# Three one-element instructions behind the last output of a two-layer feed-forward kernel

## Chip, cores and metric

The kernel runs on one core of a Trainium2 chip. The metric is the device time of one execution in microseconds (us), the median over several runs.

## The reference

`x` has 8 sequences of 128 tokens with 512 features in float32. Two layers are applied, each a conditioning projection followed by a gated feed-forward network, with the result added to `x`:

```python
x = x + _L0_ffn_ref(_L0_cond_ref(x, itok_B_0_7, W, Wr, A, B), qweight_gu, ...)
x = x + _L1_ffn_ref(_L1_cond_ref(x, weight, itok_B_3_7), ln_w, gate_w, up_w, down_w)
```

In layer 0 the conditioning is `x @ W.T` plus a low-rank term whose 8 experts are weighted by a top-2 gate; its feed-forward network has weights of 4 bits with a scale per group, width 1376. In layer 1 each sequence picks one of 8 weight matrices, the result is normalized by its root mean square, and the feed-forward network has width 1792: `(silu(g) * u) @ down_w.T`. The output has the shape of `x`.

## The kernel before

Features lie on the 128 partitions and the 1024 tokens along the free axis, in two halves of 512 (`NTB = 2`, `TB = 512`); the 512 features make four chunks (`KC = 4`). The running `x` and the final result share one tile, `xT`. Float32 products are made of several products in a faster format: each operand is split into a high part, a low part and a difference, and the sums for the high and low parts and for the differences go to one PSUM bank, which is rescaled in between.

The whole network is written by `network_in`, which the program contains twice. `adaln_ffn_kernel` first calls it in the form that the inputs normally allow (`by_groups` true). During that, a one-element count decides whether the inputs were outside what this form can take; the answer is stored in `flag`, one column of a small tile (`told`, line 974, from the 1x1 product of `met`, line 971). Behind the first network stands a conditional block, `tc.If(again[0] > 0, ...)` on line 1719, that holds the second network, a general fallback. In the runs here the block is jumped over. Every engine loads the flag (line 1641) and has its own compare-and-branch instruction on line 1719. TensorE, VectorE and ScalarE (`FETCHED`) also get a hint of the coming jump when the last down projection begins (line 1642, shown in the profile under line 1876).

The order of layer 1's work is made ahead of time by a planner (`Plan`): tasks with keys, costs and engines are sorted into one order, and each task's function writes its instructions. The last tasks are those of `down`, called for the last block of the inner dimension (`last`). There `parts` lists the eight pieces of the output, (half, feature chunk), and the last one is cut into two of 256 columns, so that `i` runs from 0 to 8 and `i == NTB * KC` is the final piece. For each piece TensorE sums products into a bank (line 1628), ScalarE or VectorE rescales it (lines 1227 and 1229), TensorE adds more, and `done` lets VectorE add the bank to `x` (line 1685) and starts the output's DMA (lines 1690 and 1692). The DMA of the last piece but one is issued from ScalarE's queue, all others from SyncE's. Behind the last piece each engine has its jump, then one instruction that waits for its own semaphore's last value and adds to it what the skipped block would have counted (line 1719), and then the closing barrier (line 1876): SyncE waits for all semaphores, every engine reports to GpSimd, and GpSimd clears the semaphores and lets all go.

Of the kernel before, what the change touches and what calls it, by code (L numbers as in the profile page):

```python
# [14 lines left out]
F32 = mybir.dt.float32  # L15
F32R = mybir.dt.float32r
I32 = mybir.dt.int32
# [4 lines left out]
ALU = mybir.AluOpType  # L22

P = 128
# [3 lines left out]
NTB = NT // TB  # L28
NWARM = 36
KC = D // P  # L30
# [70 lines left out]
GU_PLACE, FLAG_PLACE, COND_PLACE = 64, 24, 48  # L101
# [31 lines left out]
class Plan:  # L133
# [5 lines left out]
    def add(self, name, engines, fn, deps=(), key=0.0, takes=(), gives=()):  # L139
        t = Task(name, engines, fn, deps, key, takes, gives)  # L140
        for d in t.deps:
            d.then.append(t)
        self.tasks.append(t)
        return t
# [67 lines left out]
        self.us = now  # L212


def network(tc: tile.TileContext, a, out, by_groups, flag=None, again=None):


    with ExitStack() as ctx:
        network_in(ctx, tc, a, out, by_groups, flag, again)


def network_in(ctx, tc, a, out, by_groups, flag, again):
    nc = tc.nc

    const = ctx.enter_context(tc.tile_pool(name="const", bufs=1, side="left"))
# [983 lines left out]
    def of(k, *who):  # L1209
        x = plan.place[k, who]  # L1210
        return late_tiles[x] if isinstance(x, tuple) else x

    def pe(us):
        return {"pe": us}
# [7 lines left out]
    def either(n):  # L1222
        return act(n) | dve(n)

    def scaled(engine, out_, in_, by):
        if engine == "act":
            nc.scalar.activation(out_, in_, AF.Copy, scale=by)  # L1227
        else:
            nc.vector.tensor_scalar(out_, in_, by, None, ALU.mult)
# [346 lines left out]
    def h_tile(j, tb):  # L1576
        x = of("h3", j, tb)
        return x if len(x.shape) == 3 else x.rearrange("p i n k -> p i (n k)")

    def down_weights(j, k):  # L1580
        raw = add(
            "wd", {"sp": 0.4}, lambda _: nc.sync.dma_start(out=of("wd", j), in_=a["wd1"][:, j, :]), [fd_open], k - 10.0,
            [("wd", (j,))],
        )

        def high(_):
            nc.scalar.activation(of("d", j)[:, 0], of("wd", j), AF.Copy, scale=HSCALE)

        def large(_):
            nc.scalar.activation(of("wd", j), of("wd", j), AF.Copy, scale=1.0 / EPS)  # L1590

        def low(_):
            d = of("d", j)
            nc.vector.scalar_tensor_tensor(d[:, 1], d[:, 0].bitcast(F32), -1.0 / EPS, of("wd", j), ALU.mult, ALU.add)

        def diff(_):
            d = of("d", j)
            nc.vector.tensor_tensor(d[:, 2], d[:, 0].bitcast(F32), d[:, 1].bitcast(F32), ALU.subtract)

        t0 = add("d hi", act(D), high, [raw], k, [("d", (j,))])  # L1600
        t1 = add("d large", act(D), large, [t0], k)
        t2 = add("d lo", dve(D), low, [t1], k, (), [("wd", (j,))])
        t3 = add("d di", dve(D), diff, [t2], k)
        d_ready[j] = (t0, t2, t3)

    def down(j0, j1):
        k, n = begin["down", j0], j1 - j0
        last = j1 == NJ1
        for j in range(j0, j1):
            down_weights(j, k - DOWN_LEAD + D_STEP * (j - j0))  # L1610
        users = []
        parts = [(tb, m, 0, TB) for tb in range(NTB) for m in range(KC)]
        if last:
            tb, m = parts.pop()[:2]
            parts += [(tb, m, c0, c0 + TB // 2) for c0 in (0, TB // 2)]
        for i, (tb, m, c0, c1) in enumerate(parts):
            kk = k + 3 * n * PASS * i
            who = ("down", j0, m, tb, c0)
            mine, t, w = [], None, c1 - c0
            one = PASS * w / TB + (0.007 if w < TB else 0.0)  # L1620

            d_first = last and i >= NTB * KC - 1
            first_key = k + 3 * n * PASS * (NTB * KC - 1) - D_FIRST
            firsts = (2, j0) if d_first else (0, j0)

            def products(j, which, m=m, tb=tb, who=who, c0=c0, c1=c1, firsts=firsts):
                for i in which:
                    nc.tensor.matmul(  # L1628
                        of("bank", *who)[:, : c1 - c0],
                        lhsT=of("d", j)[:, i, m * P : (m + 1) * P],  # L1630
                        rhs=h_tile(j, tb)[:, i, c0:c1],
                        start=((i, j) == firsts),
                        stop=True,
                        skip_group_check=(i, j) != firsts,
                    )

            def sums(t, key, takes=()):
                for j in range(j0, j1):
                    def high_low(_, j=j, products=products, tell=(last and i == 0 and j == j0)):
                        if tell and by_groups:  # L1640
                            again.append(nc.values_load(flag[:1, :], min_val=0, max_val=1))
                            tc.mark_branch_hint_location("again", hint=again[0], engines=FETCHED)
                        products(j, (0, 1))

                    t = add(
                        "down H", pe(2 * one), high_low, [*h_ready[j, tb][:2], *d_ready[j][:2], t], key,
                        takes if j == j0 else (),
                    )
                    mine.append((j, t))
                return t  # L1650

            def differences(t, key, some, takes=()):
                def fn(_, products=products):
                    for j in some:
                        products(j, (2,))

                needs = [x[2] for j in some for x in (h_ready[j, tb], d_ready[j])]
                t = add("down D", pe(len(some) * one), fn, [t, *needs], key, takes)
                mine.extend((j, t) for j in some)
                return t  # L1660

            def rescaled(t, by, key):
                def fn(e, who=who, w=w):
                    ps = of("bank", *who)[:, :w]
                    scaled(e, ps, ps, by)

                return add("rescale", either(w), fn, [t], key)

            takes = [("bank", who)]
            if d_first:  # L1670
                t = None
                for j in range(j0, j1):
                    t = differences(t, first_key, [j], takes if j == j0 else ())
                t = rescaled(t, DSCALE, first_key)
                t = sums(t, kk)
            else:
                t = sums(None, kk, takes)
                t = rescaled(t, HLSCALE, kk + R_AT)
                t = differences(t, kk + (DD_LAST if last and i == NTB * KC - 2 else DD_AT), range(j0, j1))
            by_end = 1.0 + EPS if d_first else -EPS  # L1680

            def done(_, i=i, m=m, who=who, by_end=by_end, cols=slice(tb * TB + c0, tb * TB + c1)):
                x = xT[:, m, cols]
                ps = of("bank", *who)[:, : cols.stop - cols.start]
                nc.vector.scalar_tensor_tensor(x, ps, by_end, x, ALU.mult, ALU.add)  # L1685
                if last:
                    by = nc.scalar if i == NTB * KC - 1 else nc.sync
                    if i == 1:
                        some = out[: 2 * P, cols].rearrange("(m p) t -> p m t", p=P)
                        by.dma_start(out=some, in_=xT[:, :2, cols])  # L1690
                    elif i > 1:
                        by.dma_start(out=out[m * P : (m + 1) * P, cols], in_=x)

            add("done", dve(w), done, [t], kk + DONE_AT, (), [("bank", who)])
            users += [(j, tb, t) for j, t in mine]
        for j in range(j0, j1):
            for tb in range(NTB):
                add("h3", {None: 0.0}, None, [t for jj, tt, t in users if (jj, tt) == (j, tb)], k, (), [("h3", (j, tb))])
            add("d", {None: 0.0}, None, [t for jj, _, t in users if jj == j], k, (), [("d", (j,))])
# [11 lines left out]
@with_exitstack  # L1711
def adaln_ffn_kernel(ctx: ExitStack, tc: tile.TileContext, a, out):
    nc = tc.nc

    outer = ctx.enter_context(tc.tile_pool(name="outer", bufs=1, side="right"))
    flag = outer.tile([P, FLAG_PLACE], I32, name="flag")[:, :1]
    again = []
    network(tc, a, out, True, flag, again)
    with tc.If(again[0] > 0, preferred_fallthrough_block=True, label="again", name="again"):
        network(tc, a, out, False)  # L1720


def hidden_order(w, axis):
# [157 lines left out]
```

## Time and profile before

| | before |
|---|---|
| median of 9 runs | 414.28 us (413.5 to 414.49) |
| profiled execution, its own time | 414.49 us |
| its span, first to last instruction | 412.6 us |
| TensorE busy | 405.9 us (98%) |
| VectorE busy | 368.2 us (89%) |
| ScalarE busy | 304.4 us (74%) |
| GpSimd busy | 29.0 us (7%) |
| granted TensorE clock, mean | 0.996 |
| last VectorE instruction (line 1685) | starts at 407.51 us, takes 0.42 us |

PE is TensorE (PEld its weight loads), DVE is VectorE, ACT is ScalarE, POOL is GpSimd, SP is SyncE. A "q" behind an engine's name marks its sequencer: waits, jumps and DMA issues, in which the engine itself does nothing. Times within an execution are in us from the first instruction. Times given to a hundredth are those of the trace's own records, where a view rounds to a tenth. The profile is of one execution; the time of that execution is its span and what lies around it, here 1.9 us.

### The profile page before, as it was taken

To read this page: it belongs to the slowest core of one execution; us is meant where nothing else is said; L and a number is where in the kernel's file an instruction comes from. 1 tells how busy PE (TensorE), PEld (TensorE's weight loads), DVE (VectorE), ACT (ScalarE), POOL (GpSimd) and SP (SyncE) were. 2 spreads that over 40 slices of the span, in tenths; PEclk is the share of its full clock that TensorE was granted. 3 is DMA by queue.
4 is the path that set the end of the run, shared out by engine and by line. 5 is a ranking of instruction groups with operands and counts; after the bars stand their busy time and mean duration, and the time that the engine had idled before them with its cause. 6 is when DMAs were issued, how large, how long until landed. Compare 5 with 4: busy or idle time off the path is not lost.

```text
span 412.6 us, 5202 instructions
## 1 busy us (share of the span) xinstructions
PE 405.9 (98%) x1779; PEld 320.2 (78%) x1779; DVE 368.2 (89%) x677; ACT 304.4 (74%) x502; POOL 29.0 (7%) x35
## 2 busy tenths in 40 slices
PE   9999999999999999999999999999999999999995
PEld 9886788888888867445778888888888888888884
DVE  3998989997999788988999999989999899988973
ACT  5843688958896786487999887867976688767751
POOL 1000200000000400421011011011011101000000
PEclk9999999999999999999999999999999999999998
DMA  8930830110010540682144114323323225000005
GB/s 286 396 145 2 246 85 3 49 45 14 0 64 2 184 147 2 244 305 50 51 154 78 64 25 128 92 36 91 113 54 91 73 46 138 0 2 1 25 2 209
DMA packets 17041, 38.59 MB, mean 94 GB/s; under 512 B 1904, under 2 KB 8944, under 8 KB 15984
## 3 DMA queue, kind: packets, MB, share of 16 engines
q1 hardware_dynamic: 11472, 25.09, 18.1%
q0 software_dynamic: 5104, 12.72, 12.2%
q10 hardware_dynamic: 432, 0.39, 0.3%
q8 instruction: 15, 0.25, 0.2%
q14 instruction: 18, 0.15, 0.1%
HBM read 36.10 MB, written 2.10 MB: 93 GB/s over the span
## 4 chain that ended last, share of the span: by engine, by line
PE 91%; DVE 5%; ACT 2%; issue 0%; DVEq 0%
PE bank L1480 30%; PE bank L1628 19%; PE down L731 9%; PE gate L681 9%; PE up L681 9%; PE bank L1292 6%; PE base L532 5%; PE experts L435 2%; PE base L558 2%; PE idle L388 1%; DVE xt L1260 1%; DVE a L1257 1%; PE bank L1333 1%; DVE down L315 1%; ACT h L337 0%
## 5 line engine op out<-in xcount | busy, mean ns | idle before, releaser
L1227 ACT ACTIVATE bank<-bank 128x512 f32<-128x512 f32 (+1 forms) x126 | 71.2, 582 | 23.6 <-PE bank L1480 14.0
L1628 PE MATMUL bank<-h,d 128*128 128x512 f32 (+1 forms) x249 | 67.3, 382 | 0.0
L1628 PEld LDWEIGHTS bank<-h,d 128*128 128x128 f32 x249 | 45.6, 188 | 9.2 <-DVE h L1105 0.2
L681 PE MATMUL gate<-a,dq 128*128 128x512 f32 (+1 forms) x176 | 47.7, 393 | 0.0
L681 PE MATMUL up<-a,dq 128*128 128x512 f32 (+1 forms) x176 | 47.4, 391 | 0.0
L1480 PE MATMUL bank<-a,w 128*128 128x512 f32 x168 | 45.2, 391 | 0.4 <-ACT snap L1227 0.4
L1480 PE MATMUL bank<-xs,w 128*128 128x512 f32 x168 | 44.3, 390 | 0.0
L731 PE MATMUL down<-h,wd 128*128 128x512 f32 (+1 forms) x176 | 41.6, 391 | 0.1
L731 PEld LDWEIGHTS down<-h,wd 128*128 128x128 f32 (+1 forms) x176 | 32.9, 188 | 7.9 <-DVE h L700 0.5
L681 PEld LDWEIGHTS gate<-a,dq 128*128 128x128 f32 (+1 forms) x176 | 32.5, 185 | 8.2 <-ACT gate L313 0.6
L681 PEld LDWEIGHTS up<-a,dq 128*128 128x128 f32 (+1 forms) x176 | 32.4, 185 | 7.9 <-DVE a L824 0.3
L1480 PEld LDWEIGHTS bank<-a,w 128*128 128x128 f32 x168 | 31.2, 188 | 7.8 <-ACT snap L1227 0.8
L313 ACT ACTIVATE gate<-gate,ratio 128x1024 f32<-128x1024 f32 (+1 forms) x26 | 28.2, 1085 | 11.4 <-PE gate L681 11.4
L1480 PEld LDWEIGHTS bank<-xs,w 128*128 128x128 f32 x168 | 31.4, 188 | 6.4
L1227 ACT ACTIVATE snap<-bank 128x512 f32<-128x512 f32 x42 | 25.1, 597 | 13.6 <-PE bank L1480 13.4
L1108 DVE SCALAR_TENSOR_TENSOR w<-w 128x512 fp32r<-128x512 f32 x50 | 34.3, 687 | 0.1
L1685 DVE SCALAR_TENSOR_TENSOR xT<-bank,xT 128x512 f32<-128x512 f32 (+1 forms) x41 | 27.5, 676 | 4.2 <-PE bank L1628 3.8
L1095 POOL DMA_DIRECT2D raw<-in_wgu x14 | 17.2, 1228 | 197.6 <-PE up L681 45.9
L1514 DVE SCALAR_TENSOR_TENSOR snap<-bank,snap 128x512 f32<-128x512 f32 x42 | 28.4, 688 | 2.1 <-PE bank L1480 2.0
L1628 PE MATMUL bank<-w,d 128*128 128x512 f32 x96 | 30.1, 389 | 0.0
L1105 DVE TENSOR_TENSOR w<-raw,w 128x512 fp32r<-128x512 f32 x42 | 28.7, 686 | 0.2 <-ACT w L1102 0.2
L1292 PE MATMUL bank<-w,xT 128*128 128x512 f32 x64 | 28.9, 594 | 0.0
(169 smaller groups left out, 743.0 us busy)
## 6 DMA issues: line engine op xcount, KB each, us to landing
raw<-in_wgu SPq DMA_DIRECT2D x13, 640.0 KB, 3.9
raw<-in_wgu POOLq DMA_DIRECT2D x14, 256.0 KB, 4.5
wd<-in_wd SPq DMA_DIRECT2D x14, 256.0 KB, 2.6
qw<-in_qw_gu SPq DMA_DIRECT2D x5, 512.0 KB, 4.0
xT<-in_xT SPq DMA_DIRECT2D x2, 1024.0 KB, 12.2
xb<-in_first SPq DMA_DIRECT2D x7, 256.0 KB, 4.8
out<-xT SPq DMA_DIRECT2D x5, 256.0 KB, 2.1
qwd<-in_qw_d SPq DMA_DIRECT2D x2, 512.0 KB, 9.4
```

The lines of the kernel that those rows point to most:

```text
L313: nc.scalar.activation(ps, ps, AF.Copy, scale=by)
L532: nc.tensor.matmul(base[m], lhsT=wT3[i][:, m, c * P : (c + 1) * P], rhs=x_parts(tb)[i][:, c, :], start=(i == 0 and c == 0), stop=(i == 1 a ...
L681: nc.tensor.matmul(ps, lhsT=dqs[j][:, c, half, :], rhs=a3[i][:, c, tb * TB : (tb + 1) * TB], start=(c == 0 and i == 0), stop=(i == 1), ski ...
L731: nc.tensor.matmul(ps[:, tb], lhsT=wds[k][:n, m * P : (m + 1) * P], rhs=h2[k][i][:, tb], start=(first and i == 0), stop=(i == 1), skip_gro ...
L1105: nc.vector.tensor_tensor(lo, raw, hi.bitcast(F32), ALU.subtract)
L1108: nc.vector.scalar_tensor_tensor(di, lo.bitcast(F32), -1.0 / EPS, hi.bitcast(F32), ALU.mult, ALU.add)
L1227: nc.scalar.activation(out_, in_, AF.Copy, scale=by)
L1292: nc.tensor.matmul(of("bank", "ad", b), lhsT=xT[:, c, b * T : (b + 1) * T], rhs=of("w1", b)[:, c * D : (c + 1) * D], start=(c == 0), stop= ...
L1480: nc.tensor.matmul(ps, lhsT=w[:, i, n, c * P : (c + 1) * P], rhs=x[i][:, c0 + c], start=(first and i == which[0] and c == 0), stop=True, s ...
L1514: nc.vector.scalar_tensor_tensor(x, of("bank", j, bank_), by, x, ALU.mult, ALU.add)
L1628: nc.tensor.matmul(of("bank", *who)[:, : c1 - c0], lhsT=of("d", j)[:, i, m * P : (m + 1) * P], rhs=h_tile(j, tb)[:, i, c0:c1], start=((i, ...
L1685: nc.vector.scalar_tensor_tensor(x, ps, by_end, x, ALU.mult, ALU.add)
```

## The change

When the last piece of the output is ready, three instructions follow. TensorE makes a one-element product from the first column of that piece, into the bank that the piece has just left. ScalarE copies this element from the bank to a spare column beside the flag. VectorE multiplies it by one into the next column. Each reads what the one ahead wrote, and the first reads the last output, so the three run one behind the other. Nothing reads their result. The spare columns belong to the flag's tile, which was wide enough already. The three stand behind the issue of the last output's DMA, and they are in both copies of the network.

```diff
-def network_in(ctx, tc, a, out, by_groups, flag, again):
+def network_in(ctx, tc, a, out, by_groups, spare, flag, again):
...
                     elif i > 1:
                         by.dma_start(out=out[m * P : (m + 1) * P, cols], in_=x)
+                    if i == NTB * KC:
+                        nc.tensor.matmul(ps[:1, :1], lhsT=x[:, :1], rhs=x[:, :1], start=True, stop=True)
+                        nc.scalar.copy(spare[:1, :1], ps[:1, :1])
+                        nc.vector.tensor_scalar(spare[:1, 1:], spare[:1, :1], 1.0, None, ALU.mult)
...
-    flag = outer.tile([P, FLAG_PLACE], I32, name="flag")[:, :1]
+    flag = outer.tile([P, FLAG_PLACE], I32, name="flag")
+    spare = flag[:, 1:3].bitcast(F32)
+    flag = flag[:, :1]
     again = []
-    network(tc, a, out, True, flag, again)
+    network(tc, a, out, True, spare, flag, again)
     with tc.If(again[0] > 0, preferred_fallthrough_block=True, label="again", name="again"):
-        network(tc, a, out, False)
+        network(tc, a, out, False, spare)
```

More of the change, by code (lines that the diff above doesn't have):

```diff
@@ L212, in run, with network @@
         self.us = now
-def network(tc: tile.TileContext, a, out, by_groups, flag=None, again=None):
+def network(tc: tile.TileContext, a, out, by_groups, spare, flag=None, again=None):
     with ExitStack() as ctx:
-        network_in(ctx, tc, a, out, by_groups, flag, again)
-def network_in(ctx, tc, a, out, by_groups, flag, again):
+        network_in(ctx, tc, a, out, by_groups, spare, flag, again)
+def network_in(ctx, tc, a, out, by_groups, spare, flag, again):
     nc = tc.nc
```

## The prediction

> **What bounds the kernel now.** I read the page first, for the engine rows and the chain that ended last, then the end of the timeline, then the lines that belong to the jump over the fallback and to the closing barrier, because the change lies behind the last output and nowhere else. "About 0.2%" below is 0.83 us, roughly what a measurement of this kernel can tell from no change. The page:
>
> ```profile
> span 412.6 us, 5202 instructions
> PE 405.9 (98%) x1779; PEld 320.2 (78%) x1779; DVE 368.2 (89%) x677; ACT 304.4 (74%) x502; POOL 29.0 (7%) x35
> ...
> PE 91%; DVE 5%; ACT 2%; issue 0%; DVEq 0%
> ```
>
> TensorE sets the pace for 407.5 us. The change touches none of that: its first instruction needs the last output's tile. What counts is the stretch from the last output to the end of the span. The last rows of the timeline, with start and duration in us, then what line 1692 (the output DMAs) shows from 406.5 us on:
>
> ```profile
> 406.80 1.49 SPq L1692 DMA_DIRECT2D out<-xT  x2
> 407.25 0.36 ACTq L1692 DMA_DIRECT2D out<-xT  x1
> 407.51 0.42 DVE L1685 SCALAR_TENSOR_TENSOR xT<-bank,xT 128x256 f32<-128x256 f32 x1 [0.29 <-PE bank L1628]
> ```
>
> ```profile
> DMA to landing us min/median/max: 2.9/3.3/3.5
> ```
>
> The last output is ready at 407.93; SyncE issues its DMA at 407.96 and the trace has it landed at 410.91, 2.95 us later. The span ends at 412.61. So 4.68 us follow the last arithmetic, and none of them is an engine's work. Now the jump over the fallback (line 1719), from 407 us on: count, duration in ns, first and last start.
>
> ```profile
> L1719 SPq EVENT_SEMAPHORE  x8: 17/17/17, 408.8 to 410.9; - x8
> L1719 PEldq EVENT_SEMAPHORE  x1: 51/51/51, 407.5 to 407.5; - x1
> L1719 DVEq COMPARE_BRANCH  x1: 84/84/84, 407.5 to 407.5; - x1
> L1719 ACTq COMPARE_BRANCH  x1: 68/68/68, 407.6 to 407.6; - x1
> L1719 SPq COMPARE_BRANCH  x1: 53/53/53, 408.3 to 408.3; - x1
> L1719 ACTq EVENT_SEMAPHORE  x1: 17/17/17, 410.8 to 410.8; - x1
> L1719 DVEq EVENT_SEMAPHORE  x1: 21/21/21, 411.0 to 411.0; - x1
> ```
>
> This is the view that decides. VectorE jumps at 407.52, while its last instruction still runs, and its next record is at 411.03: 3.51 us. ScalarE jumps at 407.64 and goes on at 410.84: 3.20 us. TensorE jumped at 405.85 and was past it by 407.51, at most 1.66 us; SyncE needed 0.50 us. In between the instruction queues moved code. The DMA view from 407 us to the end:
>
> ```profile
> q14 instruction: 5, 0.04, 2.6%
> q8 instruction: 1, 0.02, 1.0%
> ```
>
> In the packets' own times q8 moves 16 KB at 407.64 for 0.88 us, q14 moves 8 KB at 408.83, 408.94 and 409.39 for 0.41 to 0.59 us. Two of these start 1.23 us after the ends of the VectorE and ScalarE jumps, so I read the 3.2 to 3.5 us as waiting for code. The hints were given at 385.2 to 385.5; no q14 packet follows until 408.83, while q8 moved 16 KB at 399.93. That fits TensorE alone finding its target loaded.
>
> Last, the closing barrier:
>
> ```profile
> L1876 SPq EVENT_SEMAPHORE  x14: 17/28/28, 411.0 to 412.5; - x14
> L1876 DVEq DRAIN  x2: 10/14/17, 411.1 to 412.1; - x2
> ```
>
> SyncE, released by the last landing at 410.91, goes through twelve checks 0.06 us apart and reports at 411.81; the rest takes a fixed 0.80 us. Its checks look at VectorE's counter at 411.55, at TensorE's at 411.61 and at ScalarE's at 411.67. VectorE's counter is right at 411.06, so VectorE has 0.49 us to spare, ScalarE 0.80 and TensorE over 4. The output's landing bounds the end, but VectorE is close behind.
>
> **The change, part by part.** Nothing is removed. No DMA moves past anything; SyncE's and GpSimd's queues keep their order. The arithmetic that is added lies beside the 2.95 us of the last landing. If it were all, it would cost nothing. But each of the three engines has its jump queued behind the new wait, and for VectorE the 3.5 us behind that jump.
>
> First, when the chain ends. For the one-column float32 matmul the trace has the same form once, line 971, two passes; the rows are from the timeline at 173 us:
>
> ```profile
> 173.35 0.09 PEld L971 LDWEIGHTS bank<-count 128*1 128x1 f32 x2 [0.76 <-issue]
> 173.35 0.19 PE L971 MATMUL bank<-count 128*1 128x1 f32 x2
> 174.16 0.14 DVE L974 TENSOR_SCALAR flag<-bank 1x1 int32<-1x1 f32 x1
> ```
>
> From the last output's end at 407.93: 0.04 until TensorE starts (what idle TensorE takes after a VectorE or ScalarE signal in this trace), 0.19 for the passes, 0.02 until ScalarE starts, 0.20 for its copy (a one-column activation of line 1407 took 203 ns), 0.02 until VectorE may start. That is 0.47, so 408.40. From above: 0.30 for a matmul out of rest (the 512-column one at 205.95, after 0.35 us idle, took 0.11 longer than its 0.39) and 0.32 for the copy (the slowest one-column root of line 1313) give 408.63. I take 408.50. VectorE's own 0.14 us lies beside its jump, as its last output does now.
>
> Second, the jumps. TensorE's moves from 405.85 to 408.0, to be done by 409.7 with its 1.66 us: nothing waits for it before 411.61. ScalarE's goes from 407.64 to about 408.2; with 3.20 us it is back at 411.4, 0.2 us before its check, and costs nothing by itself. VectorE's goes from 407.52 to 408.50. Call X what it takes from its jump to its next instruction. Its counter is right at 408.50 + X + 0.03, against the check at 411.55, so the end moves by X - 3.02 us as long as VectorE is last. With its own 3.51 us that is +0.49; with ScalarE's 3.20, +0.18. X is not shown for a jump at this time. From above: 4.4, its 3.51 and the 0.88 us of the 16 KB packet ahead of it, gives +1.4. From below: 1.31 from jump to packet, 0.31 for 8 KB (the quickest such packets took 307 ns) and 0.5 from a last packet to its signal (0.44 to 0.64 in the output DMAs here) make 2.1, or -0.9. I take 3.4, nearest to the two rows that are this very jump: +0.4 us, the span 413.0, and a profiled execution of 414.49 + 0.4 (its span and 1.9 us around it). The median was 414.28, so I forecast 414.7.
>
> [...]
>
> **The rivals.**
>
> Slower by 1 us (B). TensorE's 16 KB packet follows its jump by 1.79 us; moved to about 409.8 it meets VectorE's packet, which comes 1.31 us after its jump, also at about 409.8. Now they are 1.2 us apart. For it: output packets on a channel busy with code are visibly late (below). Against it: there are 16 channels and the two queues need not share one. Price: up to 0.88 us on X; it decides over 0.2% from X = 3.85 on. X - 3.02 is then +0.7 to +1.4; in the middle 415.3 us.
>
> Faster (C). The last output's landing is late today: 13 of its 16 shares signal by 409.70, the last three at 410.64, 410.67 and 410.91, and the code packets lie in that very stretch. With the jumps later, the output could be down at 409.7, up to 1.2 us sooner, SyncE would reach VectorE's check at 410.35, and VectorE's own wait could shrink on freed channels. For it: the late shares. Against it: VectorE is last then, and X must fall to 2.2 for 0.2%. Price 0 to -0.9; in the middle 413.8 us.
>
> Nothing moves (D). VectorE and ScalarE go on 0.12 and 0.14 us after a landing (410.91, 410.71). If the landing lets them go rather than the code, the shift is swallowed: 414.3 us. That the change doesn't do what it says hardly applies: the matmul reads the last output's tile, so it can't come earlier.
>
> **How the numbers follow.** The forecast's own case, X between 3.0 and 3.8 and 414.3 to 415.1 us, gets 0.46; B 0.29; C 0.15; D 0.10. Slower by over 0.2%: most of B and the top of the first case, 0.32. Faster by over 0.2%: most of C, 0.13. Within: 0.55. For 8 in 10 the range goes from 413.9, leaving out half of C, to 415.5, leaving out the upper third of B.
>
> **What would show it.** In the changed profile: one new chain of three at 408.0 to 408.6; TensorE's jump at 408.0, ScalarE's near 408.2, VectorE's near 408.5; VectorE's next record near 411.9, later than the last landing; SyncE's checks then waiting for it; TensorE's rows before 407.5 unchanged. I am wrong if VectorE goes on before 411.5 (C or D), if it goes on after 412.3 (B), or if anything ahead of the last output has moved.

## The result and the profile after

The changed kernel took 415.32 us in the median (10 runs, 414.57 to 415.61), against 414.13 (30 runs, 413.25 to 414.93) for the kernel before: a ratio of 1.0029 (95% interval 1.0021 to 1.0037), so 0.9 to 1.5 us slower. Two later measurements of the same program gave 1.0017 (1.0007 to 1.0027) and 1.0016 (1.0006 to 1.0027). The ratios are not the quotients of the medians, which in these two lie only 0.39 and 0.52 us above the kernel before. By the ratios the effect is 0.7 to 1.2 us; 0.65 of that is found in the traces below.

The page's head first, with the busy times of the engines, then the end of the timeline (start and duration in us):

```profile
span 412.8 us, 5208 instructions
...
PE 405.2 (98%) x1781; PEld 319.2 (77%) x1781; DVE 368.3 (89%) x678; ACT 304.7 (74%) x503; POOL 29.0 (7%) x35
```

```profile
407.10 0.42 DVE L1685 SCALAR_TENSOR_TENSOR xT<-bank,xT 128x256 f32<-128x256 f32 x1 [0.29 <-PE bank L1628]
407.55 0.33 SPq L1692 DMA_DIRECT2D out<-xT  x1
407.58 0.09 PEld L1694 LDWEIGHTS bank<-xT 128*1 128x1 f32 x2 [0.72 <-DVE xT L1685]
407.58 0.19 PE L1694 MATMUL bank<-xT 128*1 128x1 f32 x2 [0.52 <-DVE xT L1685]
407.80 0.15 ACT L1695 COPY flag<-bank 1x1 f32<-1x1 f32 x1 [2.42 <-PE bank L1694]
407.98 0.14 DVE L1696 TENSOR_SCALAR flag<-flag 1x1 f32<-1x1 f32 x1 [0.46 <-ACT flag L1695]
```

The three instructions stand one behind the other and are over 0.60 us after the last output. TensorE's busy time has not grown. By busy time the change is nothing. The jump over the fallback is now on line 1725; the rows from 407 us on, and under them SyncE's own waits in the same stretch (total us, times, longest):

```profile
L1725 PEldq COMPARE_BRANCH  x1: 397/397/397, 407.6 to 407.6; - x1
L1725 ACTq COMPARE_BRANCH  x1: 68/68/68, 407.8 to 407.8; - x1
...
L1725 DVEq COMPARE_BRANCH  x1: 84/84/84, 408.0 to 408.0; - x1
L1725 PEldq EVENT_SEMAPHORE  x1: 51/51/51, 408.1 to 408.1; - x1
L1725 ACTq EVENT_SEMAPHORE  x1: 17/17/17, 411.3 to 411.3; - x1
L1725 DVEq EVENT_SEMAPHORE  x1: 21/21/21, 411.7 to 411.7; - x1
```

```profile
SPq L1882 <- DVEq L1725: 1.8, 1, 1.8
SPq L1725 <- SPq L1725: 0.9, 2, 0.5
```

VectorE goes on at 411.69, 3.69 us after its jump. SyncE has been waiting for it since 409.98. The output is no longer what holds the end; line 1692 for the same three DMAs as before:

```profile
DMA to landing us min/median/max: 1.8/2.0/2.1
```

They land in 1.8 to 2.1 us where they took 2.9 to 3.5. The last one is down at 409.33, 1.81 us after its tile was ready (2.97 before). So a gain of 1.16 us at the landing and a new, longer wait lie in one trace, and the wait decides.

All traces can be read in one measure. Let 0 be the end of the last row of line 1685, and the tail the time from there to the end of the span. For each trace: when TensorE's, ScalarE's and VectorE's jumps start, the wait (the time from the start of ScalarE's or VectorE's jump to its next record), when VectorE goes on, when the last output lands, and the tail (all us; an experiment is named by its label).

| trace | jumps TensorE, ScalarE, VectorE | wait ScalarE, VectorE | VectorE goes on | landing | tail |
|---|---|---|---|---|---|
| before | -2.08, -0.29, -0.41 | 3.20, 3.51 | 3.10 | 2.97 | 4.67 |
| c1_before_again | -2.08, -0.29, -0.41 | 3.26, 3.53 | 3.12 | 2.85 | 4.55 |
| after | 0.05, 0.29, 0.47 | 3.48, 3.69 | 4.17 | 1.81 | 5.25 |
| a1_again | 0.05, 0.29, 0.48 | 3.55, 3.74 | 4.21 | 2.08 | 5.29 |
| d1_third | 0.05, 0.29, 0.48 | 3.59, 3.69 | 4.17 | 1.96 | 5.25 |
| a2_no_pe | -2.08, 0.04, 0.27 | 2.85, 3.03 | 3.30 | 2.95 | 4.65 |
| a3_dve_only | -2.08, -0.29, 0.05 | 3.26, 3.10 | 3.14 | 2.81 | 4.51 |
| a4_twice | 0.66, 0.89, 1.07 | 3.70, 3.69 | 4.77 | 1.83 | 5.84 |
| b1_pe_only | 0.05, -0.29, -0.41 | 3.80, 3.78 | 3.37 | 3.19 | 4.89 |
| b2_no_pe_twice | -2.08, 0.44, 0.67 | 2.59, 3.00 | 3.67 | 2.92 | 4.76 |
| b3_hint_early | -2.08, -0.29, -0.41 | 0.48, 0.60 | 0.19 | 2.77 | 4.47 |
| b4_chain_hint_early | 0.05, 0.29, 0.47 | 0.48, 0.60 | 1.07 | 1.81 | 3.51 |
| c2_chain_hint_again | 0.05, 0.29, 0.47 | 0.48, 0.60 | 1.07 | 1.81 | 3.51 |
| c3_pe_hint_early | 0.05, -0.29, -0.41 | 0.48, 0.60 | 0.19 | 3.00 | 4.70 |

Every tail is the larger of two sums, within 0.02 us: landing + 1.70, or VectorE going on + 1.07. Before, the first holds (2.97 + 1.70 = 4.67); after, the second (4.17 + 1.07 = 5.24).

The code moves through two instruction queues. In the changed kernel's trace, from 406.6 us to the end (packets, MB, share of 16 DMA engines):

```profile
q14 instruction: 5, 0.04, 3.3%
q8 instruction: 1, 0.02, 1.0%
```

On the table's scale, by the packets' own times, q8's 16 KB packet starts at -0.29 before and at 1.36 after; over all traces at -0.54 to -0.29 where TensorE jumps early and at 1.33 to 1.71 where it jumps late. Three 8 KB packets of q14 start at 0.90, 1.00 and 1.46 before and at 1.27, 1.47 and 1.57 after; two more follow once ScalarE and VectorE have gone on. In b1_pe_only the 16 KB start at 1.37 and the 8 KB at 0.92, 1.02 and 1.47; in b2_no_pe_twice at -0.52 and at 1.38, 1.47 and 1.82. A packet's record names its queue, not the engine that it is for.

### The profile page after: what moved, and what is told of

Read it like the earlier page. It is cut to its first block, busy times and chain, and to the rows that moved or that the text cites. A ratio compares the mean times of both kernels' runs of the same rounds, so it can differ in the third digit from the quotient of the medians.

```text
span 412.8 us, 5208 instructions
## 1 busy us (share of the span) xinstructions
PE 405.2 (98%) x1781; PEld 319.2 (77%) x1781; DVE 368.3 (89%) x678; ACT 304.7 (74%) x503; POOL 29.0 (7%) x35
## 4 chain that ended last, share of the span: by engine, by line
PE 90%; DVE 5%; ACT 2%; DMA 1%; issue 1%; SPq 0%; DVEq 0%
PE bank L1480 30%; PE bank L1628 19%; PE down L731 9%; PE gate L681 9%; PE up L681 9%; PE bank L1292 6%; PE base L532 5%; PE base L558 2%; PE experts L435 2%; DMA xb<-in_first 1%; DVE xt L1260 1%; DVE a L1257 1%; PE bank L1333 1%; DVE down L315 1%; ACT h L337 0%
```

## The experiments

The instructions ahead of the last output are the same, in the same order, in all kernels but the three with early hints, where only the load of the flag and the hint stand earlier. All ratios are to the kernel before on the same chip, with their 95% intervals.

**The change again (a1_again).** No edit.

> The changed kernel once more, for a second trace and a paired time. Tail means the time from the end of the last VectorE row of line 1685 to the end of the span: 4.67 us in the profile before, 5.25 in the profile after, while the median moved by 1.2 us. Theory 1 (VectorE's jump is late and its wait for code, 3.5 to 3.7 us, follows it unhidden): tail 5.1 to 5.9 here and the whole of the median's 1.2 us is to be found in the tail, so that the first trace was a short one. Rival (part of the cost lies ahead of the last output): tail again 5.25, and the median still 1.2 us above the kernel before.

Tail 5.29 us; 414.55 us against 414.16, ratio 1.0017 (1.0007 to 1.0027). The tail repeats, and it doesn't hold the first measurement's 1.2 us, as Theory 1 wanted; nor did the 1.2 us come again, as the rival had it. By the ratio the time moved by 0.7 us, about as far as the tail.

**Without TensorE (a2_no_pe).**

```diff
-nc.tensor.matmul(ps[:1, :1], lhsT=x[:, :1], rhs=x[:, :1], start=True, stop=True)
-nc.scalar.copy(spare[:1, :1], ps[:1, :1])
+nc.scalar.copy(spare[:1, :1], x[:1, :1])
```

> ScalarE copies one element of the last output itself and VectorE follows it; the TensorE product is left out, so TensorE jumps early, as before, and its 16 KB of code move before the others'. Theory 1: VectorE's jump comes 0.3 us after the last output's end instead of 0.47, its wait is 3.5 us as before, tail 4.8 to 5.0, time +0.2 to +0.4 us. Rival B (the late 16 KB packet of TensorE's code stretches VectorE's wait): the wait falls from 3.7 to 3.4 or less and the time is within 0.2 us of before. Rival (any instruction behind the last output costs the same): +1.2 us.

414.27 us against 414.16, ratio 0.9999 (0.9990 to 1.0008), tail 4.65. VectorE's jump is late by 0.68 us, yet its wait is 3.03 instead of 3.51, and the landing still sets the end. That is what rival B expected, and not Theory 1. This is the first sign that the wait behind the jump isn't a constant and that TensorE's part matters.

**VectorE alone (a3_dve_only).**

```diff
+nc.vector.tensor_scalar(spare[:1, 1:], x[:1, :1], 1.0, None, ALU.mult)
```

This line stands here in place of the three.

> Only VectorE gets an instruction, reading one element of the last output that it has itself written; TensorE and ScalarE jump as before. Its jump can only move by the 0.43 us that the last output takes. Theory 1: the move of 0.4 us is inside the 0.49 us that VectorE has to spare, tail 4.6 to 4.8, time within 0.2 us of before. Rival (any instruction behind the last output costs the same): +1.2 us.

414.04 us, ratio 0.9999 (0.9990 to 1.0008), tail 4.51. One VectorE instruction behind the last output, which moves VectorE's jump alone and by 0.46 us, costs nothing.

**The chain twice (a4_twice).**

```diff
+nc.tensor.matmul(ps[:1, :1], lhsT=spare[:1, 1:2], rhs=spare[:1, 1:2], start=True, stop=True)
+nc.scalar.copy(spare[:1, 2:3], ps[:1, :1])
+nc.vector.tensor_scalar(spare[:1, 3:4], spare[:1, 2:3], 1.0, None, ALU.mult)
```

> The chain of three twice: the second product reads the element that VectorE wrote. Theory 1: every 0.47 us on the jump is 0.47 us on the end, since nothing covers it any more; tail 5.6 to 5.8 and the time 0.4 to 0.6 us above the changed kernel, so +1.6 to +1.8 us over before. Rival (what costs is that the jumps meet on the code queues, not that they are late): no more than the changed kernel, or 0.2 us less.

415.04 us, ratio 1.0023 (1.0014 to 1.0032); the median is 0.49 us above that of a1_again, and the tail 0.55 longer, just over what Theory 1 expected. The rival is out. Over the kernel before it is 0.95 us by the ratio, not the 1.6 to 1.8 expected, since the first measurement's 1.2 us didn't come again. VectorE's jump is 0.59 us later than in the change, its wait the same 3.69, its going on 0.56 later. SyncE's wait in this trace, 1.8 us with one chain:

```profile
SPq L1885 <- DVEq L1728: 2.4, 1, 2.4
```

So with VectorE last, the 0.59 us on its jump came out as 0.55 to 0.59 us on the tail.

**TensorE alone (b1_pe_only).** The product stays, the copy and the multiplication go.

> Only the TensorE product behind the last output; ScalarE and VectorE jump early, as before, 0.3 and 0.4 us ahead of the last output's end. TensorE's jump moves to 0.05 us behind it, and its 16 KB of code from 0.3 us before to about 1.35 us after it. Theory 1: neither of the other two is late; the last output lands sooner (about 2.1 us after its tile is ready instead of 2.97), VectorE's next instruction at 3.1, tail 4.3 to 4.7, time within 0.2% of before or faster. Theory 2 (TensorE's late 16 KB stretch VectorE's wait for code): VectorE's wait grows from 3.5 to over 4 us, tail 4.7 to 5.2.

414.19 us against 414.13, ratio 1.0007 (0.9997 to 1.0016): not to be told from no change. But ScalarE's and VectorE's waits are 3.80 and 3.78 us, although both jump as early as ever. Only TensorE's jump has moved, so the longer waits are its doing. They go on at 3.5 and 3.4 us, and the landing at 3.19 sets a tail of 4.89, 0.2 to 0.3 above before. Theory 2's tail held; its wait of over 4 us didn't. Theory 1's landing at 2.1 didn't come.

**ScalarE and VectorE twice, without TensorE (b2_no_pe_twice).**

```diff
+nc.scalar.copy(spare[:1, :1], x[:1, :1])
+nc.vector.tensor_scalar(spare[:1, 1:2], spare[:1, :1], 1.0, None, ALU.mult)
+nc.scalar.copy(spare[:1, 2:3], spare[:1, 1:2])
+nc.vector.tensor_scalar(spare[:1, 3:4], spare[:1, 2:3], 1.0, None, ALU.mult)
```

> ScalarE and VectorE in turn, twice, without TensorE: VectorE's jump comes about 0.65 us after the last output's end, later than the 0.47 of the change, while TensorE's code moves early. Theory 1 with a fixed wait of 3.5 to 3.7 us: VectorE goes on at 4.2 to 4.35, tail 5.2 to 5.4, time +0.5 to +0.7 us over before. Theory 2 (the wait is 3.0 to 3.1 us unless TensorE's 16 KB come at the same time): VectorE goes on at 3.7, tail 4.7 to 4.85, time within 0.2 us of before. Theory 3 (VectorE is let go by the landing of the last output): VectorE goes on at 3.3 or sooner, tail 4.4 to 4.7.

414.33 us, ratio 1.0003 (0.9994 to 1.0012), tail 4.76. This run decides between the three. VectorE jumps at 0.67, later than in the change (0.47), and goes on earlier. Its rows, and SyncE's wait for it:

```profile
L1726 DVEq COMPARE_BRANCH  x1: 84/84/84, 408.3 to 408.3; - x1
...
L1726 DVEq EVENT_SEMAPHORE  x1: 21/21/21, 411.3 to 411.3; - x1
```

```profile
SPq L1883 <- DVEq L1726: 0.2, 1, 0.2
```

3.00 us of wait, as Theory 2 has it. Theory 1's fixed 3.5 to 3.7 is out, and so is Theory 3: VectorE goes on 0.75 us after the landing here, and 2.1 to 2.4 after it in the change.

**Early hints, no chain (b3_hint_early).** The flag is loaded and the hint given in the down projection that begins with chunk 8, not in the last. `TOLD` names VectorE and ScalarE for chunk 8 and TensorE for chunk 11, where the last one begins.

```diff
-tell=(last and i == 0 and j == j0)
+tell=(j0 in TOLD and i == 0 and j == j0)
...
-tc.mark_branch_hint_location("again", hint=again[0], engines=FETCHED)
+tc.mark_branch_hint_location("again", hint=again[0], engines=TOLD[j0])
```

> The kernel before, with the flag loaded and ScalarE's and VectorE's hints of the coming jump given one down projection earlier (at 341 instead of 385 us), ahead of the last time that their queues fetch code (362 and 374 us); TensorE's hint stays. If the hint is acted on when the next code is fetched: an extra 8 KB packet for each near 362 and 374, both engines go on within 1 us of their jump, no 8 KB packets for them during the output; tail 3.7 to 4.5, since SyncE's wait for the landing alone is left. If not: waits of 3 to 3.5 us and a tail of 4.5 to 4.8 as before.

414.01 us against 414.13, ratio 1.0001 (0.9992 to 1.0010), tail 4.47. The trace shows that TensorE's hint has moved as well: all three stand at 339.4 to 339.8 us. The waits behind the jumps are 0.48 and 0.60 us. The 8 KB packet that came at 374 us before is gone, and two come at 361.2 and 361.8 in place of one at 362; which of them holds what, the trace doesn't tell. The wait for code is gone and the time stays, because the landing (2.77) sets the end.

**The change with early hints (b4_chain_hint_early, and again as c2_chain_hint_again).**

> The changed kernel with the same early hints. Theory 1: without the wait for code the three instructions are hidden by the output's landing; with TensorE's code moved behind it too, the landing is at 1.8 to 2.1 us and the tail 3.5 to 3.8, so 0.9 to 1.2 us under the kernel before. Rival (the instructions themselves cost the time): tail 0.5 us above the kernel with early hints and no chain. If the hints are not acted on: tail 5.2 to 5.3 as in the changed kernel.

> The changed kernel with the early hints once more, since its runs fell into two groups (412.7 to 413.7 and 415.1 to 415.9 us). If its tail of 3.5 us is what the runs show, most runs lie 0.9 to 1.2 us under the kernel before. If a second group comes again, 1 to 1.8 us over it, something that the first trace doesn't show happens in some executions; a trace from that group would have a tail of 5 us or more, or a longer stretch ahead of the last output.

The jump's rows of the first of the two, and SyncE's waits, in which VectorE no longer appears:

```profile
L1726 DVEq COMPARE_BRANCH  x1: 84/84/84, 407.9 to 407.9; - x1
...
L1726 DVEq EVENT_SEMAPHORE  x1: 21/21/21, 408.5 to 408.5; - x1
```

```profile
SPq L1726 <- SPq L1726: 0.9, 2, 0.5
SPq L1693 <- DVE xT L1686: 0.7, 1, 0.7
SPq L1883 <- PEq L1883: 0.7, 2, 0.5
```

The instructions are the same three. VectorE goes on 0.60 instead of 3.69 us behind its jump, with a landing at 1.81 and a tail of 3.51 in both traces, 1.0 to 1.2 us under the kernel before. The medians are 413.58 against 414.13 and 413.61 against 414.20. The ratios are 1.0000 (0.9982 to 1.0018) and 0.9988 (0.9978 to 0.9999): the executions spread from 412.5 to 415.9 us, and 4 of 11 and 3 of 12 lie at 414.5 or above. No trace is of one of those; what happens in them is open. The second measurement's expectation fell: only 3 of its 12 executions lie 0.9 us or more under the kernel before, and its longer ones lie 0.4 to 0.7 us over it, not 1 to 1.8. So the gain is shown in the traces, and in the time only by the second measurement, by a hair.

**TensorE alone with early hints (c3_pe_hint_early).**

> Only the TensorE product behind the last output, with the early hints for ScalarE and VectorE. Nothing is late and TensorE's code comes behind the output: landing at 1.8 us, tail 3.5 us, 0.9 to 1.2 us under the kernel before. If VectorE's and ScalarE's late jumps were what helps the landing, it stays at 2.8 and the tail at 4.5.

414.48 us against 414.20, ratio 1.0007 (0.9998 to 1.0016), tail 4.70. The expectation fell: the landing is late although TensorE's code is out of the way. Line 1692 has become 1693; the last three DMAs, from 406.8 us on:

```profile
out<-xT SPq DMA_DIRECT2D x1, 256.0 KB, 2.1
out<-xT ACTq DMA_DIRECT2D x1, 128.0 KB, 2.1
out<-xT SPq DMA_DIRECT2D x1, 128.0 KB, 3.0
```

Only the last is late. ScalarE and VectorE jump early here and reach their target early; two 8 KB packets start at 0.79 and 0.88 us and take 1.21 and 1.08, so that they end at 1.99 and 1.95. The last 16 packets of output data (1 KB each) start from 1.95 on, after 0.6 us in which none starts; in the changed kernel the last one starts at 1.34. In b2_no_pe_twice it is TensorE's packet alone that comes early, and the landing is at 2.92. Over all traces, the landing is at 1.8 to 2.1 where no code packet starts between 0.6 us before and 1.2 us after the last output's end, and at 2.8 to 3.2 where one does.

**The kernel before, a second trace (c1_before_again).**

> The kernel before once more, for a second trace. If its tail (from the end of the last row of line 1685 to the end of the span) is a property of the kernel, it is again 4.5 to 4.8 us, VectorE goes on about 3.1 us after the last output and the last output lands at 2.8 to 3.0 us. If the first trace was a chance, it lies elsewhere by half a microsecond or more.

Tail 4.55, VectorE goes on at 3.12, landing at 2.85. The tail belongs to the kernel; the middle of the two is 4.61.

**The change a third time (d1_third).**

> The changed kernel a third time: its two traces so far are of executions at 414.67 and 414.33 us with tails of 5.25 and 5.29, while most executions of its first measurement lay at 415.2 to 415.6. If the extra 0.7 us of those comes from a longer wait for code behind the jump, a trace of an execution above 415 us has a tail of 5.8 to 6.2 and VectorE's or TensorE's wait longer by as much. If it lies ahead of the last output, the tail is 5.2 to 5.3 again and the last output is ready 0.5 us later or more.

414.77 us against 414.25, ratio 1.0016 (1.0006 to 1.0027). The trace is of an execution at 414.77, not of a long one, and its tail is 5.25. The question of the longer ones stays open.

## Why the prediction was right, and where it was not

The forecast of 414.7 us was short, the measured time inside its range, and the case that it held likeliest, within 0.2%, is not what the first measurement shows; the two repeats, at 0.17% and 0.16%, lie on that side of the line with intervals that cross it. The 415.32 us are the middle that it gave to rival B, but by luck: the traces find 0.65 us, nearer to the forecast's 0.4 than to B's 1.0, and where the rest of the first measurement lies stays open. Without the room that the range left for B, 415.32 would lie outside it. By its steps:

**Where the time goes: right.** It said that the three instructions are hidden by the landing and that the jumps behind them are not. a3_dve_only and a2_no_pe show the first, the after trace and a4_twice the second. VectorE's 0.49 us to spare and the formula X - 3.02 came from the profile before and hold: with the measured jump at 0.47 instead of 0.57 us after the last output the constant is 3.12, and 3.69 - 3.12 = 0.57, which is within 0.01 the difference of the first two tails (5.25 - 4.67). The mean of three tails after is 0.65 over the mean of two before, 0.16%.

**The chain's length: right, at its lower end.** 0.47 to 0.70 us from the rows, 0.57 taken, 0.47 measured. TensorE's passes took 0.19 us as in the rows. Each hand-over took 0.01 to 0.02 us more than allowed for, and the copy 0.15 us instead of 0.20; the two nearly cancel. The allowance for a matmul out of rest wasn't needed: the 0.19 us came after 0.52 us of idle TensorE.

**X, VectorE's wait behind its jump: mis-sized, for a reason near to the one that the forecast had given to a rival.** It took 3.4, because the wait had been 3.2 and 3.5 for this very jump. It was 3.69, 3.74 and 3.69: inside the 3.0 to 3.8 of the forecast's own case, and under the 3.85 from which rival B decides. What lengthens it is TensorE's late jump, with which its 16 KB come beside the others' 8 KB: the wait is 3.00 to 3.10 in the three kernels without it where VectorE jumps later than before, and 3.69 to 3.78 in the five traces with it (3.51 and 3.53 in the kernel before, where VectorE jumps earlier). That is 0.6 to 0.7 of the 0.88 us that B allowed. Neither half costs by itself. The late VectorE without TensorE would give, as an estimate from the rows of after and a2_no_pe, 0.47 + 3.03 + 1.07 = 4.57, under the landing's 4.65; TensorE's late product without the late VectorE gives a tail 0.2 to 0.3 longer that the timing doesn't resolve. It takes both, and that is what a price per part could not show.

B's own mechanism, packets that meet on a channel, isn't shown. It had put TensorE's packet 1.79 us and VectorE's 1.31 us behind their jumps; in the change they start 1.31 us and at most 1.1 us behind. They do come side by side. But how the one holds up the others isn't visible: in b1_pe_only the two earlier 8 KB packets end at 1.33 and 1.38, when the 16 KB at 1.37 have only begun, and both engines still go on later than before. In a4_twice the 8 KB packets took 0.31 and 0.47 us, no longer than in the kernel before, and VectorE still went on 2.2 us after the last of them ended.

The sum from below, 2.1 us, allowed 0.5 us from a packet's end to the engine, taken from output DMAs. The profile before already showed more: the packet that the prediction read as VectorE's ended at 409.33, and VectorE went on at 411.03, 1.70 us later. What fills that time no trace shows.

**Rival C: its first half right.** The landing moved from 2.97 and 2.85 to 1.81 to 2.08, as the thirteen punctual shares had suggested. X didn't fall with it, so VectorE took the end. The gain comes out only where VectorE finds its code (b4_chain_hint_early).

**Rival D: out.** VectorE goes on 2.1 to 2.4 us after the last landing.

**Hints and the time of the last fetch: right as far as tested.** The prediction read the hints at 385 us as too late for all but TensorE. Given at 339.4 to 339.8 us, before the last fetch of code, they cut ScalarE's and VectorE's waits to 0.48 and 0.60 us. Without that the waits were 2.59 to 3.80 us, and the 8 KB packets took only 0.3 to 0.9 us of it. That these are waits for code is a reading of the packets that lie in them and of the runs with early hints; no record shows the cause itself. The records of the jumps don't hold the time: ScalarE's is 68 ns, VectorE's 84 and TensorE's 397 with early hints (b4_chain_hint_early) as without (after).

**Open.** The first measurement's median is 1.19 us over before, of which the tails explain 0.65. Its profiled execution took 414.67 us, nearly its fastest. The last output's end varies from 406.87 to 407.93 us over the traces with no order by kernel, so the rest may lie ahead of the tail or in tails that no trace caught.

## What to carry to other kernels

An instruction placed last can cost what is queued behind it: here a jump and 3.7 us of waiting for code, of which about 0.6 us show at the end, and not its own 0.15 us. One instruction on VectorE alone cost nothing (ratio 0.9999, a tail of 4.51 us against 4.67 and 4.55). At a kernel's end, read for each engine when it jumps, when its next record comes and what the closing barrier waits for last, and take the end as the larger of those sums. A change that shortens one of them alone may show nothing: in b3_hint_early VectorE went on at 0.19 us instead of 3.10, and the ratio was 1.0001; with the landing at 1.81 as well, in b4_chain_hint_early, the tail fell to 3.51. Count code packets as transfers: here the last output landed at 2.77 to 3.19 us where one started beside it, and at 1.81 to 2.08 where none did.

## What the runs showed of the hardware that was not expected

The wait for code behind a jump isn't fixed: 2.59 to 3.80 us for the same 8 KB in the two engines, longest when TensorE's 16 KB were fetched in the same microsecond. The last output's DMA is late where code is fetched beside it: its 128 KB landed 1.81 to 2.08 us after the tile was ready where no code packet started between 0.6 us before and 1.2 us after that, and at 2.77 to 3.19 where one did. With its hint given at 340 us and new code fetched at about 344, 370 and 399 us, TensorE still went on 0.45 to 0.46 us after its late jump near 407 (0.46 to 0.53 with the hint at 385); whether it needs the hint no run shows.
